# Paged attention behind three conditional layers: page numbers read two batches ahead on the SP queue, new values loaded in a batch's sixth step, output-weight loads in other steps

## The chip, the cores and the metric

The kernel runs on one core of one Trainium2 chip. The metric is the device time of one execution in microseconds (us). Before the change three runs took 1156.72, 1157.05 and 1160.14 us; their median is 1157.05 us. The profile was taken in an execution of its own.

## The reference

32 sequences ("batches") of 32 tokens pass through three layers that pick their weights by index, and then through attention over a paged cache. Only the attention is touched by the change:

```python
q = jnp.einsum('bsd,ed->bse', x, Wq).reshape(bsz, seqlen, HQ, D)   # 32 heads of 128
k = jnp.einsum('bsd,ed->bse', x, Wk).reshape(bsz, seqlen, HK, D)   # 8 key heads
v = jnp.einsum('bsd,ed->bse', x, Wv).reshape(bsz, seqlen, HK, D)
...
kc = k_cache[block_table].reshape(bsz, L, HK, D)                   # 16 pages of 32 keys each
vc = v_cache[block_table].reshape(bsz, L, HK, D)
...
scores = jnp.einsum('bqhd,bkhd->bhqk', q, k_all) * SCALE
scores = jnp.where(valid[:, None, None, :], scores, -1e+30)
probs = jax.nn.softmax(scores, axis=-1)
o = jnp.einsum('bhqk,bkhd->bqhd', probs, v_all)
return jnp.einsum('bse,de->bsd', o.reshape(bsz, seqlen, HQ * D), Wo)
```

`block_table[b]` lists the 16 cache pages of batch b. `k_all` and `v_all` are the cached keys and values with the 32 new ones behind them, 544 in all. Everything is float32.

## The kernel before

The first part (up to about 373 us) computes the three layers and the projections. The new queries, keys and values go to scratch arrays in DRAM (`q_d`, `k_d`, `v_d`). The attention then runs as one loop of 264 steps, n = 0 to 263. Step n belongs to batch b = n // 8 and key head g = n % 8. In each step TensorE (PE) computes the scores of (b, g) in two products (L1011 for nine pages, L1012 for seven pages and the new keys), one or two of the 32 head products of an output tile that is being finished (L1166, from n = 37 on), and the weighted values of step n - 8 (L1089; the constant LAG is 8). Until n = 36 some steps also hold a piece of the last value projection (L313), whose results are stored to `v_d`. VectorE, ScalarE and GpSimd turn scores into placed, transposed probabilities in between.

In this loop the order on every engine is the order in which the code is written (`manual_schedule`), the SP queue included. SP issues the DMAs of the keys, queries, new values, page tables and output weights, one after the other; an instruction of SP that waits holds back all that stand behind it. In the built program each DMA of SP also waits until the one issued eight places earlier has landed.

What SP does for batch b, before the change:

- Step 0: `load_queries(b, 1)` (`qt`, L229, the second half of the queries; its buffer is that of the batch before, so it waits for the last scores of batch b - 1). Then `load_new_values(b)` (`vn`, L265, four DMAs of 32 KB). Then `Picked(...)` for batch b + 1: it reads the first eight page numbers from the table in SBUF into registers of SP (eight register loads, L187). Then the new keys of batch b + 1 (`kt`, L224), and pages 0 to 11 of batch b + 1 (`kt`, L199, 128 KB each); after each of the first eight pages the next page number is read.
- Step 4: the first half of the queries of batch b + 1 (`qt`, L229; it waits for the scores of step 3), its inverse roots (`rq`, L235), pages 12 to 15 (L199), and the table of batch b + 2 (`pages`, L172, 64 bytes).
- Steps listed in `WO_AT`: one of the output weights' 32 loads (`wo`, L910). The first 16 bring the heads 0 to 19 (320 KB each), the other 16, in steps 40 to 55, the heads 20 to 31 (192 KB each). Load i of the first 16 holds a quarter of the rows of the heads h with h % 4 = i // 4, so the last four (12 to 15) are needed for heads 3, 7, 11 and so on. The first heads are used in step 37 (head 0), 38 (head 1) and 39 (heads 2 and 3).

Keys of batch b + 1 overwrite those of batch b - 1 (two buffers, `home_0` and `home_1`). The new values `vn` have two buffers too; `vn` of batch b is read in step 8b + 11. Cached values (`vt`, L253) are gathered by GpSimd on a queue of its own, in steps 0 to 3 of their batch, and first read in step 8b + 8.

Of the kernel before, what the change touches and what calls it, by code (L numbers as in the profile page):

```python
# [21 lines left out]
B, S, HID = 32, 32, 512  # L22
D, HQ, HK = 128, 32, 8
REP = HQ // HK
PAGES, PSIZE, NPP = 64, 32, 16
# [13 lines left out]
QUAD = 4  # L39
# [20 lines left out]
def cond_resid_kernel(  # L60
# [18 lines left out]
    nc = tc.nc  # L79
# [86 lines left out]
    pages_of = {}  # L166

    def load_table(b: int):

        pages_of[b] = const.tile([1, NPP], I32, tag="pages", name=f"pages_{b}", bufs=4)  # L170
        at = B + b * NPP
        nc.sync.dma_start(out=pages_of[b], in_=pick[:, at : at + NPP])  # L172
# [36 lines left out]
    def load_keys(b: int):  # L209

        pool = homes[b % 2]
        kt = pool.tile([P, NPP + 1, HK * PSIZE], F32, tag="kt", name=f"kt_{b}")
        kts[b] = kt
# [9 lines left out]
    def load_new_keys(b: int):  # L223
        nc.sync.dma_start(out=kts[b][:, NPP, :], in_=k_d[b])  # L224

    def load_queries(b: int, q: int):

        qts[b, q] = qp.tile([P, HALF * S], F32, tag="qt", name=f"qt_{b}_{q}")
        nc.sync.dma_start(  # L229
            out=qts[b, q], in_=q_d[b][:, q * HALF * S : (q + 1) * HALF * S]  # L230
        )

    def load_inverses(b: int):
        rqs[b] = const.tile([P, 2, QUAD], F32, tag="rq", name=f"rq_{b}", bufs=2)
        nc.sync.dma_start(out=rqs[b], in_=r_d[:, b * S : (b + 1) * S])  # L235

    def page_keys(b: int):
        return [kts[b][:, n, :] for n in range(NPP)]

    K_SHAPE = "a d x -> d (a x)"  # L240
# [8 lines left out]
    def load_value_chunk(b: int, c: int):  # L249
        if c == 0:  # L250
            vts[b] = homes[b % 2].tile([P, L // P, HK * D], F32, tag="vt", name=f"vt_{b}")
        at = b * (L // P) + c
        nc.gpsimd.indirect_dma_start(  # L253
            out=vts[b][:, c, :],
            out_offset=None,
            in_=v_cache,
            in_offset=bass.IndirectOffsetOnAxis(ap=v_idx[:, at : at + 1], axis=0),
        )

    def load_new_values(b: int):  # L260

        vn = vnp.tile([P, HK // QUAD, D], F32, tag="vn", name=f"vn_{b}")
        vns[b] = vn
        for u in range(QUAD):
            nc.sync.dma_start(  # L265
                out=vn[u * S : (u + 1) * S, :, :],
                in_=v_d[b * S : (b + 1) * S, :].rearrange("s (q u d) -> u s q d", u=QUAD, d=D)[u],
            )
# [53 lines left out]
    def store_values(vs, c: int, t: int, eng):  # L322
        c0 = (c - (HQ + HK) // REP) * HID
        eng.dma_start(out=v_d[t * P : (t + 1) * P, c0 : c0 + HID], in_=vs)
# [676 lines left out]
    def quad_of(b: int, g: int):  # L1001
        return b, g // QUAD

    def scores(b: int, g: int):
        kt, qt = kts[b], qts[quad_of(b, g)]
        kt4 = kt.rearrange("d n (h o) -> d n h o", h=HK)

        ps = ps_s.tile([P, 2 * L], F32, tag="s", name=f"s_ps_{b}_{g}")
        u = g % QUAD
        q = qt[:, u * REP * S : (u + 1) * REP * S]  # L1010
        nc.tensor.matmul(ps[:, first:L], q, kt4[:, :N_LOW, g, :], start=True, stop=True)  # L1011
        nc.tensor.matmul(  # L1012
            ps[:, L : first + LT], q, kt4[:, N_LOW:, g, :], start=True, stop=True
        )
        if u == 0:
            prs[quad_of(b, g)] = tp.tile([P, QUAD, LT], F32, tag="pr", name=f"pr_{b}_{g}")
        pr = prs[quad_of(b, g)][:, u, :]
        low = tp.tile([P, 1], F32, tag="low", name=f"low_{b}_{g}", bufs=4)

        nc.vector.tensor_tensor_reduce(  # L1020
            pr,
            ps[:, first : first + LT],
            mask,
            rqs[b][:, g // QUAD, u : u + 1],
            3.0e38,
            ALU.add,
            ALU.min,
            low,
        )
        return b, g, pr, low  # L1030

    def exponentials(b: int, g: int, pr, low):
        quad, u = quad_of(b, g), g % QUAD
        if u == 0:
            dens[quad] = tp.tile([P, QUAD], F32, tag="den", name=f"den_{b}_{g}", bufs=4)
        nc.scalar.activation(  # L1036
            pr, pr, AF.Exp, bias=low, scale=-1.0, accum_out=dens[quad][:, u : u + 1]
        )
# [97 lines left out]
    def flip_kept(n: int):  # L1136

        while kept and kept[0][3] <= n:
            b, q, o, _ = kept.pop(0)
            t, j = divmod(b, BT)  # L1140
            if (t, q) not in ots:
                i = (2 * t + q) % 3
                ots[t, q] = places[i].tile(
                    [P, HALF, P], F32, tag=f"ot_{i}", name=f"ot_{t}_{q}", bufs=1
                )
            nc.vector.transpose(  # L1146
                ots[t, q][:, :, j * S : (j + 1) * S],
                o.rearrange("p (k d) -> p k d", d=S),
            )
# [3 lines left out]
    def load_residual(t: int):  # L1153
        x3s[t] = tp.tile([P, HID], F32, tag="os", name=f"x3_{t}")
        nc.sync.dma_start(out=x3s[t], in_=x_d[t])
# [61 lines left out]
    FILLED = 37  # L1217
    EMPTY = tuple(n for n in range(LAG + 2, FILLED) if n % 2 == 0)
    EMPTY = EMPTY[: FILLED - len(fills)]
    filled, unstored = {}, {}  # L1220
    WO_AT = list(range(6, FILLED, 2)) + list(range(FILLED + 3, FILLED + 3 + REP * REP))

    def fill(n: int):
        if n < FILLED and n not in EMPTY:
            t, k = fills.pop(0)
            if k == 0:
                filled[t] = ps_p.tile([P, HID], F32, tag="f", name=f"qkv_{NCH - 1}_{t}")
            project_part(filled[t], NCH - 1, t, k)
            if k == KC - 1:
                unstored[n + 2] = copy_values(filled.pop(t), NCH - 1, t), NCH - 1, t, nc.sync  # L1230
# [8 lines left out]
    with tc.manual_schedule(engines=order):  # L1239
        for n in range(N + LAG):  # L1240
            b, g = divmod(n, HK)
            if n == FILLED + 2:
                pa.close()
                late = ctx.enter_context(tc.tile_pool(name="b_w", bufs=1))
                places.append(late)
                wos[1] = late.tile([P, LATE, HID], F32, name="wo_1")
            if BEGIN <= n <= N and n % (BT * HK) == 0:

                load_residual((n - BEGIN) // (BT * HK))
            if n < N:  # L1250
                if g == 0 and b >= 1:
                    load_queries(b, 1)
                    load_new_values(b)
                if g == 0 and 1 <= b < B - 1:
                    load_keys(b + 1)
                    keys = Picked(nc.sync, k_cache, pages_of.pop(b + 1), page_keys(b + 1), K_SHAPE)
                    load_new_keys(b + 1)
                    keys.transfer(slice(0, 12))
                if g < L // P and b >= 2:
                    load_value_chunk(b, g)  # L1260
                if g == QUAD and b < B - 1:
                    load_queries(b + 1, 0)
                    load_inverses(b + 1)
                    if b >= 1:
                        keys.transfer(slice(12, NPP))
                    if 1 <= b < B - 2:
                        load_table(b + 2)
                scored = scores(b, g)
                exponentials(*scored)
            flip_kept(n)  # L1270
            fill(n)
            if n in unstored:
                store_values(*unstored.pop(n))
            if n == QUAD + 1:
                load_new_values(0)
            if n in WO_AT:
                i, part = divmod(WO_AT.index(n), REP * REP)
                load_wo(i, *divmod(part, REP))
            if QUAD <= n < N + QUAD:
                bq, i = divmod(n - QUAD, HK)  # L1280
                q, j = divmod(i, QUAD)
                if j == 0:
                    gather_new(bq, q)
                if j == 2:
                    flip_new(bq, q)
                place(bq, q, j)
            share(n)
            if n >= LAG:
                values(*units[n - LAG])
            if n < N and g == HK - 1 and b < B - 1:  # L1290
                see_keys(b + 1)
            if n > N + QUAD:
                at = 4 * (n - N - QUAD - 1)
                finish(NT - 1, range(at, at + 4))
        assert not dens and not prs and not pos and not placed and not pns
        load_residual(NT - 1)
        flip_kept(N + LAG)
        finish(NT - 1, range(3 * QUAD, HALF))
        finish_by_halves(NT - 1)
# [76 lines left out]
```

## Time and profile before

| | us |
|---|---|
| median of the three runs | 1157.05 |
| the profiled execution | 1152.46 |
| its span, first to last instruction | 1150.4 |
| busy in the span: PE | 1127.8 |
| DVE | 805.5 |
| ACT | 751.8 |
| POOL | 553.1 |
| first scores of the attention (L1011) | 373.6 |
| mask of batch 5, 6, 7, 8 (L219, start) | 490.95, 514.59, 536.42, 559.52 |
| mask of batch 10, 11, 12, 13, 14 | 606.65, 628.48, 650.49, 674.34, 697.62 |

The mask of a batch is made once, at its beginning, so the distance between two masks is one batch: 21.8 to 23.9 us late in the loop, in a pattern that repeats every four batches (four output tiles' steps). The chain of waits that ended last runs through PE. Of the idle time of PE before L1012, 6.4 us in three waits ended with a DMA of cached keys; before L1011 it was 1.2 us. The SP rows of the timeline show the DMAs' issue alone: a row's duration is the time that issuing took, and register loads do not appear, so that their time is a gap between two rows.

### The profile page before, as it was taken

The page shows a single profiled execution, that of the slowest core. Times are in us where ns is not written, and L with a number is a line of the kernel's source. Part 1 is how long each engine was busy: PE and PEld are TensorE (multiplying, and loading weights), DVE is VectorE, ACT ScalarE, POOL GpSimd, SP SyncE. Part 2 cuts the span into 40 slices and gives each one's busy share as a digit, 9 for nine tenths or more (in the row PEclk, how much of TensorE's full clock was granted, in tenths as well). Part 3 has the DMA queues.
Part 4 walks back from the last instruction along what each step waited for, and adds up shares of the span by engine and source line. Part 5 has one row for each costly group of instructions (what it writes and reads, how often), then busy time and mean ns, then how long its engine had stood idle before and what let it go on. Part 6 is the DMA issues. An engine that isn't in the chain of part 4 may idle for free. (4 is left out here: it accounts for less than half of the span.)

```text
span 1150.4 us, 19414 instructions
## 1 busy us (share of the span) xinstructions
PE 1127.8 (98%) x5432; PEld 733.4 (64%) x5432; DVE 805.5 (70%) x1670; ACT 751.8 (65%) x1900; POOL 553.1 (48%) x709
## 2 busy tenths in 40 slices
PE   8999999999999988899999999999999999999998
PEld 5454444444444566677777777777777777777766
DVE  2510688897876577678868877877777777877861
ACT  1212378666666777767777877777777877787750
POOL 3410689898988434343344334533443444344410
PEclk9999999999999999999999999999999999999999
DMA  8998447656366499989766776776677767775700
GB/s 317 393 411 338 176 134 233 167 150 175 91 178 166 119 270 269 271 234 291 249 211 206 256 235 201 225 253 214 213 227 236 232 205 223 246 232 190 246 29 10
DMA packets 170510, 250.88 MB, mean 218 GB/s; under 512 B 31362, under 2 KB 130306, under 8 KB 164642
## 3 DMA queue, kind: packets, MB, share of 16 engines
q1 hardware_dynamic: 147586, 167.44, 47.0%
q0 software_dynamic: 19216, 69.35, 17.9%
q10 hardware_dynamic: 3600, 12.85, 3.2%
q8 instruction: 44, 0.72, 0.3%
q14 instruction: 64, 0.52, 0.1%
HBM read 220.07 MB, written 29.49 MB: 217 GB/s over the span
## 5 line engine op out<-in xcount | busy, mean ns | idle before, releaser
L1061 ACT COPY placed<-turned 32x512 f32<-32x512 f32 x539 | 332.1, 616 | 31.4 <-DVE turned L1049 23.3
L1089 PEld LDWEIGHTS o_ps<-vt,placed 128*128 128x128 f32 x2048 | 269.2, 193 | 115.4 <-issue 89.7
L1020 DVE CUSTOM_DVE_ANT_0 pr<-s_ps,mask,rq 128x544 f32<-128x544 f32 x256 | 200.6, 784 | 140.8 <-PE s_ps L1012 132.9
L1036 ACT ACTIVATE pr<-pr,low 128x544 f32<-128x544 f32 x256 | 191.7, 749 | 145.2 <-DVE low L1020 143.2
L1089 PE MATMUL o_ps<-vt,placed 128*128 128x128 f32 x2048 | 271.9, 276 | 3.2 <-DVE ot L1146 1.3
L1063 POOL COPY placed<-turned 32x512 f32<-32x512 f32 x268 | 162.9, 608 | 231.4 <-DVE turned L1049 177.0
L1166 PE MATMUL f_ps<-wo,ot 128*128 128x512 f32 x480 | 242.0, 595 | 3.5 <-issue 2.8
L1049 DVE STREAM_TRANSPOSE turned<-pr 128x512 f32<-128x512 f32 x256 | 178.7, 698 | 0.1
L1011 PE MATMUL s_ps<-kt,qt 128*128 128x288 f32 x512 | 175.4, 424 | 1.8 <-DMA kt<-in_k_cache_dram 1.2
L1012 PE MATMUL s_ps<-kt,qt 128*128 128x256 f32 x512 | 153.1, 381 | 6.8 <-DMA kt<-in_k_cache_dram 6.4
L253 POOL DMA_INDIRECT vt<-in_v_cache_dram,v_idx x128 | 126.9, 991 | 39.3 <-issue 23.5
L1012 PEld LDWEIGHTS s_ps<-kt,qt 128*128 128x128 f32 x512 | 97.3, 191 | 35.2 <-issue 7.8
L432 POOL TENSOR_TENSOR ra<-ra,rs 128x512 f32<-128x512 f32 x80 | 103.7, 1302 | 10.9 <-DVE rs L427 9.3
L1166 PEld LDWEIGHTS f_ps<-wo,ot 128*128 128x128 f32 x480 | 85.7, 190 | 31.7 <-issue 17.0
L1065 DVE COPY placed<-turned 32x512 f32<-32x512 f32 x217 | 94.5, 435 | 5.5
L1072 POOL COPY pq<-pr 128x128 f32<-128x128 f32 x64 | 18.4, 288 | 164.1 <-PE o_ps L1089 90.3
L1011 PEld LDWEIGHTS s_ps<-kt,qt 128*128 128x128 f32 x512 | 77.8, 192 | 18.2 <-DVE low L1020 10.8
L445 ACT ACTIVATE sq<-x 128x128 f32<-128x128 f32 x256 | 76.2, 300 | 16.2 <-DVE x L403 12.8
L542 ACT COPY r<-m 128x512 f32<-128x512 f32 x80 | 46.3, 580 | 55.2 <-PE m L387 54.2
L387 PE MATMUL m<-w_pair,x3t 128*128 128x512 f32 x160 | 75.2, 592 | 0.0
L387 PE MATMUL m<-t_pair,x_sums 128*128 128x512 f32 x160 | 75.2, 592 | 0.0
L387 PE MATMUL m<-w_pair,x_sums 128*128 128x512 f32 x160 | 72.2, 592 | 0.0
(128 smaller groups left out, 1218.2 us busy)
## 6 DMA issues: line engine op xcount, KB each, us to landing
kt<-in_k_cache_dram SPq DMA_DIRECT2D x512, 128.0 KB
wa<-in_w_adapt_dram SPq DMA_DIRECT2D x32, 1024.0 KB
q_d<-st SPq DMA_DIRECT2D x128, 128.0 KB
qt<-q_d SPq DMA_DIRECT2D x64, 256.0 KB
w_pair<-in_w_qkv_dram ACTq DMA_DIRECT2D x8, 1024.0 KB
wo<-in_w_o_dram SPq DMA_DIRECT2D x16, 320.0 KB
k_d<-st SPq DMA_DIRECT2D x32, 128.0 KB
kt<-k_d SPq DMA_DIRECT2D x32, 128.0 KB
```

What stands on the lines that cost most here:

```text
L253: nc.gpsimd.indirect_dma_start(out=vts[b][:, c, :], out_offset=None, in_=v_cache, in_offset=bass.IndirectOffsetOnAxis(ap=v_idx[:, at : at ...
L387: nc.tensor.matmul(ps, of[:, k], by[:, k], start=(not more and k == 0), stop=(k == KH - 1), skip_group_check=more,)
L432: nc.gpsimd.tensor_tensor(u.a, u.a, u.s, ALU.add)
L1011: nc.tensor.matmul(ps[:, first:L], q, kt4[:, :N_LOW, g, :], start=True, stop=True)
L1012: nc.tensor.matmul(ps[:, L : first + LT], q, kt4[:, N_LOW:, g, :], start=True, stop=True)
L1020: nc.vector.tensor_tensor_reduce(pr, ps[:, first : first + LT], mask, rqs[b][:, g // QUAD, u : u + 1], 3.0e38, ALU.add, ALU.min, low,)
L1036: nc.scalar.activation(pr, pr, AF.Exp, bias=low, scale=-1.0, accum_out=dens[quad][:, u : u + 1])
L1049: nc.vector.transpose(part, pr)
L1061: nc.scalar.copy(dst, src)
L1063: nc.gpsimd.tensor_copy(dst, src)
L1089: nc.tensor.matmul(po, pt[:, c, :], vt[:, c, g * D : (g + 1) * D], start=(c == 0 and q == 0), stop=(c == L // P - 1 and q == 1),)
L1166: nc.tensor.matmul(pfs[t][:, :HID], ots[t, h // HALF][:, h % HALF, :], wo(h), start=(h == 0), stop=(h == (HQ if t < NT - 1 else HALF) - 1),)
```

## The change

```diff
-    WO_AT = list(range(6, FILLED, 2)) + list(range(FILLED + 3, FILLED + 3 + REP * REP))
+    WO_AT = [6, 7, 11, 13, 14, 15, 17, 19, 21, 22, 23, 27, 29, 30, 31, 35]
+    WO_AT += range(FILLED + 3, FILLED + 3 + REP * REP)
...
                 if g == 0 and b >= 1:
                     load_queries(b, 1)
-                    load_new_values(b)
                 if g == 0 and 1 <= b < B - 1:
                     load_keys(b + 1)
-                    keys = Picked(nc.sync, k_cache, pages_of.pop(b + 1), page_keys(b + 1), K_SHAPE)
                     load_new_keys(b + 1)
+                    keys.dsts = page_keys(b + 1)
                     keys.transfer(slice(0, 12))
...
+                if g == QUAD + 1 and b >= 1:
+                    load_new_values(b)
+                if g == QUAD + 2 and b < B - 2:
+                    keys = Picked(nc.sync, k_cache, pages_of.pop(b + 2), range(NPP), K_SHAPE)
```

FILLED is 37, QUAD 4, NPP 16 and B 32. The first eight register loads for the keys of batch b + 2 now stand in step 6 of batch b, ahead of the step in which those keys are issued (step 0 of batch b + 1); the pages' destinations are filled in there. `vn` of batch b is loaded in step 5 instead of step 0. The first 16 output-weight loads stand in the steps listed: two in batch 0, four in batch 1, five in batch 2, four in batch 3 and one (step 35) in batch 4, where there were 1, 4, 4, 4 and 3. The second 16 stay in steps 40 to 55. On PE, DVE, ACT and POOL the instructions and their order are the same as before; only SP's order differs.

## The prediction

> **What bounds the kernel now.** First the page: which engine fills the span, and how full are the 16 DMA engines over it?
>
> ```profile
> span 1150.4 us, 19414 instructions
> ...
> PE 1127.8 (98%) x5432; PEld 733.4 (64%) x5432; DVE 805.5 (70%) x1670; ACT 751.8 (65%) x1900; POOL 553.1 (48%) x709
> ...
> DMA  8998447656366499989766776776677767775700
> ...
> q1 hardware_dynamic: 147586, 167.44, 47.0%
> q0 software_dynamic: 19216, 69.35, 17.9%
> ```
>
> TensorE leaves 1150.4 - 1127.8 = 22.6 us idle, so no change that only reorders SP can give more than about that. The DMA row is at 9 in slices 15 to 17 (403 to 489 us: batches 1 to 4) and at 6 or 7 in most of what follows. Whether SP's order matters can differ between these two stretches, so I read both. Second, PE's timeline, for the places where it stood still in the attention:
>
> ```profile
> 413.32 0.72 PE L1011 MATMUL s_ps<-kt,qt 128*128 128x288 f32 x2 [0.88 <-DMA kt<-in_k_cache_dram]
> 416.12 1.19 PE L1012 MATMUL s_ps<-kt,qt 128*128 128x256 f32 x2 [2.08 <-DMA kt<-in_k_cache_dram]
> ...
> 440.83 0.67 PE L1012 MATMUL s_ps<-kt,qt 128*128 128x256 f32 x2 [2.41 <-DMA kt<-in_k_cache_dram]
> ...
> 463.72 0.67 PE L1012 MATMUL s_ps<-kt,qt 128*128 128x256 f32 x2 [1.87 <-DMA kt<-in_k_cache_dram]
> ...
> 487.02 1.57 PE L1166 MATMUL f_ps<-wo,ot 128*128 128x512 f32 x2 [2.82 <-issue]
> ```
>
> These are steps 16, 24 and 32 (the first of batches 2, 3 and 4), where the last cached keys came late, and step 39. There the profile names no releaser. But it is the second head product of that step, head 3, which needs the last of the first 16 `wo` loads, and SP's rows show that one issued 4.3 us before. Third, SP's timeline, there and for one late batch:
>
> ```profile
> 482.66 0.35 SPq L910 DMA_DIRECT2D wo<-in_w_o_dram  x1
> ...
> 701.43 0.35 SPq L224 DMA_DIRECT2D kt<-k_d  x1
> 702.01 9.71 SPq L199 DMA_DIRECT2D kt<-in_k_cache_dram  x12
> 711.81 0.38 SPq L229 DMA_DIRECT2D qt<-q_d  x1
> ...
> 713.12 1.89 SPq L199 DMA_DIRECT2D kt<-in_k_cache_dram  x4
> 715.10 0.28 SPq L172 DMA_DIRECT2D pages<-in_pick_dram  x1
> 717.08 0.34 SPq L229 DMA_DIRECT2D qt<-q_d  x1
> 717.47 2.48 SPq L265 DMA_DIRECT2D vn<-v_d  x4
> 722.96 0.34 SPq L224 DMA_DIRECT2D kt<-k_d  x1
> ```
>
> Between `qt` and the new keys lie 2.48 us of `vn` issue and a gap of 722.96 - 719.95 = 3.01 us: the eight register loads, 0.38 us each. The keys could go 722.96 - 717.5 = 5.4 us earlier. Fourth, the windows, cut where PE resumed (columns: stretch, length, busy and count of PE, PEld, DVE, ACT, POOL, clock, DMA share, GB/s):
>
> ```profile
> 390.00:413.30 23.30, 21.94 (x126) 15.92 (x125) 15.27 (x34) 18.52 (x39) 13.34 (x23) 1.00 0.60 172
> 413.30:440.80 27.50, 22.02 (x124) 17.07 (x125) 18.05 (x39) 18.85 (x38) 10.81 (x18) 0.94 0.92 262
> 440.80:463.70 22.90, 20.47 (x122) 15.67 (x123) 17.66 (x38) 17.98 (x36) 8.92 (x14) 1.00 0.94 276
> 463.70:490.10 26.40, 23.42 (x127) 17.42 (x128) 16.37 (x36) 17.88 (x36) 8.37 (x13) 0.95 0.88 267
> ...
> 606.30:628.20 21.90, 21.90 (x130) 16.71 (x129) 18.17 (x39) 17.48 (x36) 9.31 (x15) 1.00 0.70 230
> ```
>
> Batches 2 to 4 keep the DMA engines 88 to 94% busy; batch 1 leaves 40% free; a late batch has PE busy for all of its 21.9 us. So there are two regimes: late, nothing that SP does is waited for; early, the keys wait partly for SP's order and partly for the DMA engines themselves.
>
> **What the stalls cost.** Each is measured from one step's L1011 to the next, against the same kind of step undisturbed. A step without a third product takes 404.77 - 402.70 = 2.07 us. Step 16: 418.81 - 412.44 = 6.37, lost 4.3 (2.96 of waiting, and matmuls that took about twice as long after it: granted clock 0.50 in 416 to 418). Step 24: 442.38 - 437.77 = 4.61, lost 2.5. Step 32: 465.27 - 461.14 = 4.13, lost 2.1. Step 39: 490.09 - 482.26 = 7.83 against 2.77 for a step with one head plus 0.86 for the second, lost 4.2. By the masks, batch 5 took 23.64 us where batch 9 took 23.28, and batch 7 23.10 where batch 11 took 22.01: 0.4 + 1.1 more. From batch 8 on the pattern repeats to 0.1 us. All of it is 14.6 us, the ceiling of the change.
>
> **The change, part by part.** *Register loads and `vn` out of step 0.* No issue is removed: 2.48 + 3.01 = 5.5 us of SP's time per batch move behind the table's load. In a late batch SP's work is `qt` 0.4, new keys and twelve pages 10.4, `qt` and `rq` 1.3, four pages 2.0, table 0.4, `vn` 2.5, registers 3.0 = 20.0 us of 21.8; it still fits, with 1.8 us to spare. There the last page was issued at 715.0 and read at 719.1 without a wait, so pages 3 to 5 us earlier give nothing: 0 for batches 8 to 31. The work that hides the moved `vn` is the six steps between 8b + 5 and 8b + 11 (six by 2.7 = 16 us; before eleven steps). Its buffer was last read in step 8b - 5, so no wait is added there.
>
> *A new wait.* The first register load waits for the table issued in step 4; before, it stood eight steps' worth of work later. In a late batch `vn` covers 2.5 us of the landing, and SP's spare 1.8 us and the 4.1 us of the pages' old lead cover more; I cost it at 0. Queued behind it are the second query half, the new keys and all pages, and `wo` and `v_d` stores early on. No row shows the table's landing. The nearest are the gathers of 512 KB, 3.9 to 8.7 us with a median of 6.5; as 64 bytes it should be near or below the lower one, but behind pages in a full queue it lands with them.
>
> *Step 16 (batch 1).* SP ended `vn` of batch 0 at 387.2. The register loads now follow (to 390.2), two `wo` (0.9), `qt` (0.4): new keys at 391.7 instead of 395.8, 4.1 us earlier, into engines that are 60% busy. Two `wo` that stood ahead of the last pages (405.3, 406.3) become one. The last page needs to land 3.7 us earlier (416.1 to 412.4). I take the whole 4.3 us back; the bounds are 2.5 (a slow step still follows) and 4.3.
>
> *Step 24 (batch 2).* Steps 13 to 15 put two `wo` and a `v_d` store ahead of the keys, and batch 2 has five `wo` instead of four. Bytes that must land from about 412.5 on: two `wo` 0.66 MB, `v_d` 0.26, two `qt` 0.52, seventeen key pieces 2.23, cached values 2.10, two more `wo` 0.66: 6.43 MB. At 262 GB/s for 0.92 busy, 0.285 MB per us, that is 22.6 us: 435.1, and 1.5 to 2.3 us for landing (the fastest gather, 3.9 us, less 0.52 MB at q0's 0.337 MB per us), so about 437. Without a stall step 24 would be ready near 433.2 (412.4 + 20.8). So about 3.7 us are waited, 1.2 more than before. Bounds: 2.5 back (if the weights' bytes are absorbed) and 2.5 more lost (with a slowed clock). I take -1.2. *Step 32:* four `wo` as before, pages started about 2.5 us earlier against its step; +1.0 of 2.1, bounds -1 and 2.1. *Step 39:* the last load moves from behind the four pages of batch 4 to before its `qt`, 482.66 to near 476 on the old clock; +4.2, bounds 2 and 4.2. *Step 40:* its keys follow three `wo` left by batch 3; -1.0, bounds -2 and 0. *Batches 5 to 7:* same `wo` as before, pages earlier: +1.4, bounds 0 and 1.5.
>
> One page speaks against all of this. The Trainium skill ("DMA: Bandwidth & Descriptors", section "Issuing engines are not separate DMA queues") says that DMAs from every engine run on the same 16 DMA engines and interleave, and that issuing differently saves only the sequencer's time. The rows agree for batches 2 to 4 (0.88 to 0.94 busy) and not for batch 1 (0.60). By that rule alone steps 24 and 32 would give nothing, and the sum would be 4.3 + 4.2 + 1.4 - 1.0 = 8.9 us; with SP's issue taken as the only limit it would be the 14.6 us.
>
> **The sum.** 4.3 - 1.2 + 1.0 + 4.2 - 1.0 + 1.4 = 8.7 us off the profiled 1152.46 (span 1150.4 and 2.1 around it): 1143.8. The median of the runs is 4.6 us above that execution; the same difference gives 1157.05 - 8.7 = **1148.4 us**.
>
> **The rivals.** *SP's issue was the only limit:* nearly all stalls vanish, 12 to 14.6 us, 1142.5 to 1145. For it: even in the full stretch the share dips to 0.58 and 0.72 at 426 to 430 while SP issues pages. Against it: 22 to 25 us of DMA work per batch in 21 us of PE work. *The stalls only move:* batches 2 to 4 take as long as their bytes, batch 1's gain is waited for again at step 24 or 28 (the query half now stands behind the register loads), and only step 39 or part of it remains: within 3.5 us of before, about 1155. Against it: batch 1's free 40%, 9 us. *The table's wait becomes the lock (slower):* SP sits at the first register load until the table lands, and every page of the next batch behind it. Place: step 6 of each batch. Late in the loop the table would be issued 14.4 us into SP's batch of 21.8, and before, the pages began 5.9 us after `qt`; so pages are later than now only if the table takes over 21.8 + 5.9 - 0.6 - 3.0 - 14.4 = 9.7 us, and PE waits only after 1 to 2 us more. At 12 us, 1 us in each of 24 batches, less 8.7: 1172. For it: in the full stretch pages landed 5.5 to 6.5 us after their issue. Against it: late the engines are 70% busy, and 600 to 606 us, where a batch's loads have ended, shows a share of 0.30.
>
> **How the numbers follow.** Forecast 60%, between 1145 and 1153; all stalls gone 17%; stalls moved 15%; lock 8%. The range takes in the second case and most of the third: 1142 to 1156. A difference under 0.3% (3.5 us, 1153.6 to 1160.5) is about what these runs can tell from none. The first two cases lie below it: faster 0.77, same 0.15, slower 0.08.
>
> **What would show it.** In the profile after: no wait of PE for `kt` at step 16 and none at head 3 of step 39; `qt` of step 0 followed at once by the new keys; a wait for `kt` of 1 to 4 us left at step 24; batches from 8 on as long as before to 0.1 us; a gap of about 3 us behind `vn` in step 6, longer in batches 1 to 4. I am wrong if step 16 still waits for keys, if step 24 doesn't, or if late batches lengthen.

## The result and the profile after

The change made the kernel slower. Six runs of the changed kernel took 1167.02 to 1174.56 us, median 1170.85; six runs of the kernel before, taken beside them, 1156.67 to 1160.14, median 1157.55. The ratio is 1.0113, with a 95% interval of 1.0088 to 1.0139: about 13 us lost, where the forecast was 8.7 us gained. One run of those reported below (1166.50 us, of e2_new_wo_alone) fell into a slower state and is left out of its figures. The profiled execution is the one of 1167.02 us. From its page, the span, the engines and the DMA row:

```profile
span 1165.2 us, 19419 instructions
...
PE 1133.3 (97%) x5432; PEld 734.2 (63%) x5432; DVE 804.5 (69%) x1670; ACT 751.5 (65%) x1900; POOL 552.8 (47%) x709
...
DMA  8998456646376688789775776677577766766610
```

TensorE is still busy nearly all the time, but its idle time grew from 22.6 to 31.9 us (1165.2 - 1133.3), and its busy time by 5.5 us, although the matmuls are the same. Of these 5.5 us, 1.5 lie in batches 0 to 7, where some matmuls run slowly after a long wait, as the rows below show; 3.4 lie in batches 8 to 31 and 0.5 ahead of the attention. Where it happened is told by two stretches of equal length in both kernels, in the view by windows (columns: stretch, length, busy time and count of PE, PEld, DVE, ACT, POOL, then the granted clock, the DMA share, GB/s). The kernel before:

```profile
374.00:562.00 188.00, 174.55 (x951) 128.04 (x950) 132.46 (x287) 137.31 (x282) 75.53 (x118) 0.98 0.83 240
562.00:1140.00 578.00, 575.83 (x3261) 428.54 (x3260) 438.41 (x934) 424.67 (x849) 224.23 (x335) 1.00 0.65 210
```

The changed kernel:

```profile
374.00:562.00 188.00, 167.20 (x898) 121.23 (x897) 125.20 (x271) 130.02 (x273) 69.35 (x108) 0.97 0.83 233
562.00:1140.00 578.00, 575.13 (x3260) 427.06 (x3260) 442.77 (x947) 433.08 (x866) 230.58 (x345) 1.00 0.65 213
```

In the first stretch (batches 0 to 7 of the kernel before) TensorE did 53 matmuls fewer in the same 188 us and lost 7.3 us of work; the DMA engines are as busy as before but moved 233 GB/s instead of 240. In the second stretch TensorE lost only 0.7 us of 578. So the added waiting lies in the first eight batches. Five of the longer waits in TensorE's timeline of the changed kernel there (in brackets: the wait, and what ended it):

```profile
426.47 0.72 PE L1011 MATMUL s_ps<-kt,qt 128*128 128x288 f32 x2 [1.17 <-DMA qt<-q_d]
...
439.94 1.30 PE L1011 MATMUL s_ps<-kt,qt 128*128 128x288 f32 x2 [3.65 <-DMA kt<-in_k_cache_dram]
...
454.43 0.72 PE L1011 MATMUL s_ps<-kt,qt 128*128 128x288 f32 x2 [2.20 <-DMA qt<-q_d]
...
481.26 1.30 PE L1011 MATMUL s_ps<-kt,qt 128*128 128x288 f32 x2 [5.45 <-DMA qt<-q_d]
...
543.14 0.72 PE L1011 MATMUL s_ps<-kt,qt 128*128 128x288 f32 x2 [2.05 <-DVE mask L219]
```

The waits at steps 16 and 39 are gone. New ones ended with `qt<-q_d`: the second half of the queries, at steps 20, 28 and 36 (step 4 of batches 2, 3 and 4). No such wait was there before. Step 24 waits longer than before (3.65 us; 2.41 before). Two rows show 1.30 us for a pair of products that takes 0.72 us elsewhere; the granted clock was 0.50 there, from 440 to 442 and from 481 to 483 us. The row at 543.14 (step 56) names VectorE, whose mask was done at 542.42; by the trace of the DMAs' landings the first query half of that batch, issued behind four `wo`, landed at 543.05. Step by step, from the start of L1011 in a step to that in the next, the two profiled executions differ like this (worked out from the two traces; minus is gained):

| steps | what waits there | after - before, us |
|---|---|---|
| 15, 16 | cached keys, batch 2 | -3.5 |
| 19, 20 | query half, batch 2 | +0.2 |
| 23 to 25 | cached keys, batch 3 | +2.7 |
| 27, 28 | query half, batch 3 | +1.8 |
| 32, 33 | cached keys, batch 4 | -1.5 |
| 35, 36 | query half, batch 4 | +7.0 |
| 39 | output weights, head 3 | -4.3 |
| 40 to 63 (batches 5, 6, 7) | query halves, keys, weights | +6.3 |
| batches 8 to 31 | (below) | +4.1 |

With 0.2 us in other steps these make the 13.0 us by which the attention became longer. Another 1.7 us lie ahead of it, where nothing was changed.

**Why the query half was late at step 36.** SP's timeline before, from the table of batch 5 to the keys:

```profile
458.55 0.28 SPq L172 DMA_DIRECT2D pages<-in_pick_dram  x1
460.06 1.15 SPq L910 DMA_DIRECT2D wo<-in_w_o_dram  x2
461.31 0.39 SPq L324 DMA_DIRECT2D v_d<-vs  x1
461.80 0.38 SPq L229 DMA_DIRECT2D qt<-q_d  x1
462.22 2.55 SPq L265 DMA_DIRECT2D vn<-v_d  x4
467.77 0.34 SPq L224 DMA_DIRECT2D kt<-k_d  x1
```

and after:

```profile
462.65 0.28 SPq L172 DMA_DIRECT2D pages<-in_pick_dram  x1
462.98 2.68 SPq L265 DMA_DIRECT2D vn<-v_d  x4
465.70 3.66 SPq L910 DMA_DIRECT2D wo<-in_w_o_dram  x2
469.47 0.38 SPq L324 DMA_DIRECT2D v_d<-vs  x1
469.90 0.43 SPq L910 DMA_DIRECT2D wo<-in_w_o_dram  x1
470.42 0.38 SPq L229 DMA_DIRECT2D qt<-q_d  x1
470.85 0.57 SPq L224 DMA_DIRECT2D kt<-k_d  x1
```

From the table to `qt` SP took 461.80 - 458.55 = 3.25 us before and 470.42 - 462.65 = 7.77 after. The row of 3.66 us for two `wo` holds the register loads between them. Before, `qt` was issued ahead of the four gathers of cached values (the first at 462.61). After, it came behind all four (465.56 to 469.61), three `wo` and a store of 256 KB. In the trace of the DMAs' landings it landed 5.3 us after its issue before, and 10.7 us after it now, at 481.12; TensorE resumed at 481.26. Meanwhile the DMA engines had had time to spare, as the windows of the changed kernel show:

```profile
462.00:464.00 2.00, 2.00 (x13) 1.47 (x11) 1.46 (x4) 1.95 (x6) 1.17 (x2) 1.00 0.91 269
464.00:466.00 2.00, 1.68 (x7) 0.66 (x5) 1.31 (x3) 1.96 (x4) 1.67 (x3) 1.00 0.17 50
466.00:468.00 2.00, 1.81 (x12) 1.71 (x13) 1.97 (x4) 0.93 (x3) 1.76 (x3) 1.00 0.58 131
468.00:470.00 2.00, 2.00 (x13) 1.50 (x12) 1.92 (x6) 1.46 (x3) 1.42 (x2) 1.00 1.00 265
```

While SP issued four small `vn` loads and read registers, the DMA share fell to 0.17 and 0.58. Behind that the loads came in one heap. The same place before (461 to 467 us, in three windows of 2 us) kept 0.97, 0.96 and 1.03.

### The profile page after: what moved, and what is told of

It reads as the page before. It is cut to its first block, busy times and chain, and to the rows that moved or that the text cites. A ratio compares the mean times of both kernels' runs of the same rounds, so it can differ in the third digit from the quotient of the medians.

```text
span 1165.2 us, 19419 instructions
## 1 busy us (share of the span) xinstructions
PE 1133.3 (97%) x5432; PEld 734.2 (63%) x5432; DVE 804.5 (69%) x1670; ACT 751.5 (65%) x1900; POOL 552.8 (47%) x709
## 5 line engine op out<-in xcount | busy, mean ns | idle before, releaser
L1011 PE MATMUL s_ps<-kt,qt 128*128 128x288 f32 x512 | 177.0, 428 | 16.3 <-DMA qt<-q_d 9.7
L1011 PEld LDWEIGHTS s_ps<-kt,qt 128*128 128x128 f32 x512 | 77.9, 192 | 33.9 <-issue 12.4
```

## The experiments

Theory A: the loss comes from the new steps of the output weights, which together with the value stores stand ahead of the query half. Theory B: it comes from moving the register loads and the new values. All ratios below are against runs of the kernel before on the same chip.

| run | median us (range) | before there | ratio [95% interval] |
|---|---|---|---|
| e1_old_wo | 1163.41 (1161.38 to 1165.95) | 1153.94 | 1.0087 [1.0062, 1.0111] |
| e2_new_wo_alone | 1156.35 (1145.84 to 1159.04) | 1153.94 | 1.0004 [0.9974, 1.0033] |
| e3_vn_alone | 1154.65 (1151.94 to 1160.34) | 1153.94 | 1.0011 [0.9992, 1.0031] |
| e4_registers_alone | 1165.89 (1163.17 to 1167.57) | 1153.94 | 1.0111 [1.0085, 1.0137] |
| r1_after_again | 1170.05 (1168.07 to 1170.98) | 1154.44 | 1.0145 [1.0127, 1.0164] |
| r2_undo_registers | 1156.01 (1151.53 to 1161.39) | 1154.44 | 1.0019 [1.0000, 1.0038] |
| r3_extra_registers | 1162.52 (1159.46 to 1164.64) | 1154.44 | 1.0076 [1.0058, 1.0093] |
| r4_after_gathers_later | 1167.06 (1163.22 to 1172.19) | 1154.44 | 1.0122 [1.0099, 1.0146] |
| t1_registers_table_early | 1161.62 (1154.31 to 1169.68) | 1156.46 | 1.0036 [1.0011, 1.0060] |
| t2_after_table_early | 1170.41 (1165.77 to 1174.07) | 1156.46 | 1.0114 [1.0084, 1.0143] |
| w1_weights_in_batch0 | 1154.50 (1150.97 to 1159.60) | 1156.46 | 0.9983 [0.9965, 1.0001] |
| w2_plus_first_registers | 1155.22 (1150.16 to 1159.06) | 1156.46 | 0.9979 [0.9961, 0.9996] |
| e4_again | 1165.90 (1162.37 to 1170.22) | 1154.21 | 1.0103 [1.0079, 1.0127] |
| t1_again | 1162.31 (1152.97 to 1166.50) | 1154.21 | 1.0052 [1.0026, 1.0078] |
| x5_early_table_old_values | 1162.93 (1160.59 to 1165.24) | 1154.21 | 1.0080 [1.0059, 1.0100] |
| x4_registers_from_batch7 | 1156.43 (1155.25 to 1163.47) | 1154.21 | 1.0033 [1.0017, 1.0050] |

### The parts by themselves

`e1_old_wo` is the changed kernel with the old steps of the output weights:

```diff
-    WO_AT = [6, 7, 11, 13, 14, 15, 17, 19, 21, 22, 23, 27, 29, 30, 31, 35]
-    WO_AT += range(FILLED + 3, FILLED + 3 + REP * REP)
+    WO_AT = list(range(6, FILLED, 2)) + list(range(FILLED + 3, FILLED + 3 + REP * REP))
```

> The change with the old list of output-weight steps (6, 8, ... 36), so that only the register loads and the new values are moved. Theory A (the loss comes from output-weight loads and value stores that now stand ahead of the second query half and the keys at a batch's beginning): the early loss of about 9 us by batch 8 goes, 1155 to 1161 us, and the wait for the second query half at steps 20, 28 and 36 shrinks below 1 us each. Theory B (moving the register loads and new values is itself the loss, because the pages are now issued while the cached values' gathers run): 1165 to 1172 us, with the waits at steps 20, 28 and 36 still there. Both expect the 0.4 to 0.6 us per four batches of the late loop to remain (3 to 4 us in all).

`e2_new_wo_alone` is the kernel before with the new list alone, the reverse of that diff.

> Before with the new list of output-weight steps alone. Theory A: slower, 1160 to 1168 us, since the loads of steps 13 to 15, 21 to 23 and 29 to 31 stand ahead of the queries and keys here too; late batches as before to 0.1 us. Theory B: 1153 to 1159 us, the stall at step 39 gone (4 us) and no new one.

`e3_vn_alone` is the kernel before with the new values in step 5:

```diff
                     load_queries(b, 1)
-                    load_new_values(b)
...
+                if g == QUAD + 1 and b >= 1:
+                    load_new_values(b)
```

> Before with the new values loaded in step 5 instead of step 0; register loads and output weights as before. Pages start 2.5 us earlier. Theory A: 1152 to 1158 us. Theory B: part of the late loss, about half of 0.55 us per four batches, and no loss early: 1157 to 1161 us.

`e4_registers_alone` is the kernel before with the first eight register loads in step 6:

```diff
-                    keys = Picked(nc.sync, k_cache, pages_of.pop(b + 1), page_keys(b + 1), K_SHAPE)
                     load_new_keys(b + 1)
+                    keys.dsts = page_keys(b + 1)
...
+                if g == QUAD + 2 and b < B - 2:
+                    keys = Picked(nc.sync, k_cache, pages_of.pop(b + 2), range(NPP), K_SHAPE)
```

> Before with the first eight register loads moved to step 6; new values and output weights as before. Pages start 3 us earlier, and the second query half stands behind the register loads, which wait for the table. Theory A: 1152 to 1159 us. Theory B: 1159 to 1166 us, with a wait of over 1 us for the second query half in at least one of the steps 20, 28 and 36.

The register loads alone cost as much as the whole change (1.0111). The new list alone and the new values alone change the median by less than can be told. Theory A falls as the main cause. Of Theory B only the register loads are left: e3 stayed at 1154.65 us where it asked for 1157 to 1161, and e1, at 1163.41, lies between the ranges of both theories. All four profiles lose in batches 1 to 8 only; from batch 9 on each batch takes as long as before to 0.01 us, so that the late loss of 3 to 4 us that both theories expected of e1 is not there.

The waits do not go the way the time goes. In e1 TensorE waits less than 1 us for the query half at steps 20, 28 and 36, as Theory A asked, and its profile is 13.2 us behind that of before at batch 8 all the same: it waits 3.87 us at step 39 and 5.03 us at step 59. In e2 the stall at step 39 shrank to 0.51 us, but 6.06 us are waited for cached keys at step 32, where Theory B expected no new stall.

In e4's trace SP stood at the first register load until the table had landed: SP's waits name this 29 times, 42.7 us in all. At the end of batch 2 the table was issued at 438.02 and landed at 439.82, and the loads ended at 442.5. The query half came 443.43 - 438.02 = 5.4 us behind the table; before it was 437.96 - 434.67 = 3.3. Theory C from here: the loads in step 6 hold SP for 3 to 4 us, ahead of output weights, value store and query half.

### The same again, one part undone, waits alone, gathers later

`r1_after_again` is the changed kernel once more.

> The changed kernel once more, on another run of the chip. Theory C (the eight register loads in step 6 hold SP for 3 to 4 us in front of the output weights, the value store and the second query half of the same batch, which then reach the full DMA engines together with the gathers; only the stretch up to batch 8 pays): ratio to before 1.008 to 1.014, and batches 8 to 31 as long as before to 0.1 us each, so that the 0.4 us at step 4 of every fourth late batch in the first profile belonged to that execution. Rival L (the register loads cost something in late batches too): the same 0.4 us at step 4 of batches 10, 14, 18, 22, 26, 30 again.

The loss came again, 1.0145 (just above Theory C's range), and again at steps 28 and 36 (waits of 3.81 and 5.46 us for `qt`). In batches 8 to 31 it was 0.9 us in all, 0.33 of it at batch 8, against 4.1 us in the first profile; the 0.4 us at step 4 of every fourth batch was not there. The same 0.4 us turned up later in the profiles of t1 (first run, not the second), t2, w1 and w2; w1 has nothing of the change but other steps for the first weights. So it comes and goes between executions of one kernel, and is not the change's; where it comes from stays open.

`r2_undo_registers` is the changed kernel with the register loads back in step 0:

```diff
                     load_keys(b + 1)
+                    keys = Picked(nc.sync, k_cache, pages_of.pop(b + 1), page_keys(b + 1), K_SHAPE)
                     load_new_keys(b + 1)
-                    keys.dsts = page_keys(b + 1)
...
-                if g == QUAD + 2 and b < B - 2:
-                    keys = Picked(nc.sync, k_cache, pages_of.pop(b + 2), range(NPP), K_SHAPE)
```

> The changed kernel with the first eight register loads back in step 0 of the batch; new values in step 5 and the new output-weight steps stay. Theory C: the loss goes with them, ratio to before 0.996 to 1.004. Rival (the three parts hurt only together): ratio above 1.006.

1.0019: the loss is gone with the one part. A long wait stays, in TensorE's timeline of this run:

```profile
437.28 1.04 PE L1011 MATMUL s_ps<-kt,qt 128*128 128x288 f32 x2 [2.81 <-DMA kt<-in_k_cache_dram]
...
454.92 1.30 PE L1011 MATMUL s_ps<-kt,qt 128*128 128x288 f32 x2 [5.28 <-DMA qt<-q_d]
```

So step 28's wait for the query half does not need the register loads; it is longer than with them (2.20 and 3.81 us in the two profiles of the change). The new values (step 21) and three `wo` (steps 21, 22, 23) stand right ahead of it there, and this gives back much of what steps 16 and 39 bring; with the new list alone (e2) the same wait was 1.08 us. At step 36, though, nothing is waited for: `qt` was issued at 468.11 and landed at 476.50, 8.4 us later, where the changed kernel took 10.7 and 12.0 us in its two profiles. TensorE also came to this batch later than in the changed kernel, by 2.9 and 1.7 us (the table at the end of the experiments).

`r3_extra_registers` is the kernel before with eight more register loads in step 6:

```diff
+                if g == QUAD + 2 and b < B - 2:
+                    Picked(nc.sync, k_cache, pages_of[b + 2], range(NPP), K_SHAPE)
```

> The kernel before with eight more register loads in step 6, whose values are not used; the eight of step 0 stay. Theory C (SP held in step 6 is the price): ratio 1.007 to 1.014, with PE waiting for the output weights at step 39 for 5 to 7 us, as where the loads were moved. Rival D (what hurts is that step 0 no longer has the pause of 3 us, so that pages run into the gathers): within 0.3% of before.

This run told something else than was meant. The values of the extra loads are not used, and in the built program the loads are gone; what is left is an empty instruction for each, 0.06 us apart, with the wait of the first one. So it is the wait for the table and half a microsecond more, and its ratio is 1.0076. The stall at step 39 grew to 5.31 us, as Theory C asked. SP's waits, of the kernel before (columns: waited for, us in all, times, longest):

```profile
SPq L229 <- PE s_ps L1012: 66.3, 30, 4.8
```

and of this run:

```profile
SPq L187 <- DMA pages<-in_pick_dram: 38.8, 29, 1.9
...
SPq L229 <- PE s_ps L1012: 8.3, 12, 1.9
```

A wait of 38.8 / 29 = 1.3 us per batch was enough. In the late batches it cost little (0.9 us in batches 8 to 31 in all): there SP had been waiting for TensorE at the query half anyway, 66.3 us in 30 waits in the kernel before, which are now 8.3 us.

`r4_after_gathers_later` is the changed kernel with the gathers one step later:

```diff
-                if g < L // P and b >= 2:
-                    load_value_chunk(b, g)
+                if 1 <= g <= L // P and b >= 2:
+                    load_value_chunk(b, g - 1)
```

> The changed kernel with the four gathers of cached values one step later (steps 1 to 4 of a batch instead of 0 to 3). Theory C with the gathers as the competitor: the query half lands before them, PE's waits for qt at step 4 of batches 2, 3 and 4 (1.2, 2.2 and 5.5 us in the first profile after) fall to a third or less in sum, and the ratio to before is at most 1.006. Rival (the bytes alone set the length of batches 2 to 4): the waits move to other steps and the ratio stays at 1.009 to 1.014.

The waits for `qt` at steps 20, 28 and 36 fell to 3.56 + 2.86 = 6.4 us from 9.3 in the run of the changed kernel on this chip, not to a third, and the ratio stayed at 1.0122. That gathers come first is a part of the delay, but moving them does not give the time back; the rival was nearer.

### Without the wait for the table, and two other lists

`t1_registers_table_early` is e4 with this besides:

```diff
-                    if 1 <= b < B - 2:
-                        load_table(b + 2)
+                    if b < B - 3:
+                        load_table(b + 3)
```

> Only the register loads are moved to step 6, as in the run of that part alone, but the table they read is loaded one batch earlier (step 4 of the batch before), so that it has landed long before. Theory W (the wait for the table is most of the price: SP may not issue until the table, and with it what stands ahead of it in the queue, has landed, and the DMA engines run low meanwhile; in the run with extra register loads the build had dropped the unused loads and kept their waits, and that alone gave 1.0076): ratio to before at most 1.005. Rival H (each microsecond for which SP is held in step 6 costs the same, waiting or loading; 2.7 us of the 3.5 to 4 are loads): ratio 1.006 to 1.010.

`t2_after_table_early` is the changed kernel with the same.

> The changed kernel with the table loaded one batch earlier. Theory W: ratio to before at most 1.006 and waits for qt at step 4 of batches 2 to 4 of less than 5 us in sum (9 to 11 us in the two profiles of the change). Rival H: ratio 1.008 to 1.012, waits of 6 us or more.

`w1_weights_in_batch0` is the kernel before with `WO_AT = [4, 5, 6, 7, 12, 13, 14, 15, 16, 18, 20, 22, 24, 26, 28, 30]` for the first sixteen.

> The kernel before with the first sixteen output-weight loads in steps 4 to 7, 12 to 15 and then every second step from 16 to 30, so that four lie in batch 0 and none in batch 4; nothing else moved. If batches 2 to 4 are long because of what SP's queue and the DMA engines have to do there, the wait at step 39 (4.2 us) goes and step 16 gives 0 to 2 us: ratio 0.994 to 0.998. Rival (what is taken from step 39 is waited for elsewhere, as in the run of the change's new list alone): 0.999 to 1.003.

`w2_plus_first_registers` is the same with the first register loads for batch 2 in step 6 of batch 0 and all others in step 0:

```diff
+                    if b >= 2:
-                    keys = Picked(nc.sync, k_cache, pages_of.pop(b + 1), page_keys(b + 1), K_SHAPE)
+                        keys = Picked(nc.sync, k_cache, pages_of.pop(b + 1), page_keys(b + 1), K_SHAPE)
+                    keys.dsts = page_keys(b + 1)
...
+                if n == QUAD + 2:
+                    keys = Picked(nc.sync, k_cache, pages_of.pop(2), range(NPP), K_SHAPE)
```

> The same with the register loads for the keys of batch 2 alone in step 6 of batch 0, where the table landed long ago and SP has room. The wait at step 16 (4.3 us) goes as well, as wherever SP reached those keys 3 us earlier: ratio 0.990 to 0.996. Rival (the gain of step 16 is waited for again at step 24): no better than the run without it.

For the loads alone the early table took most of the price away (1.0036); for the whole change it took nothing (1.0114). There, the four `vn` loads stand between table and register loads and cover the landing: SP's waits in the changed kernel have no line for L187 at all, so that there was nothing to remove. In the full change theory W falls and rival H holds.

The two lists win little. w1's profile has no wait at steps 16 and 39, which together are 8.5 us, and these in their place:

```profile
437.90 1.09 PE L1011 MATMUL s_ps<-kt,qt 128*128 128x288 f32 x2 [2.24 <-DMA kt<-in_k_cache_dram]
...
466.18 1.19 PE L1012 MATMUL s_ps<-kt,qt 128*128 128x256 f32 x2 [3.64 <-DMA kt<-in_k_cache_dram]
```

What is saved at steps 16 and 39 is waited for again at steps 24 and 32. Both ratios miss the gains expected (0.994 to 0.998 and 0.990 to 0.996). At 0.9983 and 0.9979 the two are the fastest versions here, but only the second one's interval lies below 1, by less than the 0.3% that counts as a difference.

### What settles it

`e4_again` and `t1_again` are the two runs of the moved loads, with the late and the early table, on one chip.

> The register loads alone in step 6 once more, now beside the same with an early table on one chip. All theories: ratio to before 1.008 to 1.014.

> The register loads alone in step 6, table loaded one batch earlier, once more. Theory W (alone, the wait for the table is most of the price): at most 1.006 and at least 0.004 below the run with the late table on this chip. Rival H (time of SP is time of SP, waiting or loading): within 0.003 of it.

1.0103 and 1.0052, or 12 and 6 us: about half goes with the wait, the rest stays (two thirds in the first pair of runs, 1.0111 and 1.0036, which were on different chips). T1_again is 0.0051 below e4_again, as theory W asks, and still above the kernel before, so the loads have a price of their own. SP's waits of e4_again:

```profile
SPq L187 <- DMA pages<-in_pick_dram: 41.0, 29, 2.9
```

In t1_again this line is not there. In both the largest stall of TensorE is the one at step 39 for the last output weights (2.82 us before). In the timeline of e4_again:

```profile
493.86 2.04 PE L1166 MATMUL f_ps<-wo,ot 128*128 128x512 f32 x2 [6.00 <-issue]
```

and of t1_again:

```profile
492.82 2.05 PE L1166 MATMUL f_ps<-wo,ot 128*128 128x512 f32 x2 [7.05 <-issue]
```

In e4_again the last of the first sixteen, in step 36, was issued at 490.14, where it had been 482.66 (2.0 us of this lie ahead of the attention), and landed at 493.77. So the loads alone act at step 39, through the output weights; in the full change they act at step 36, through the query half.

`x5_early_table_old_values` is t2 with the new values back in step 0.

> The changed kernel with the table one batch earlier and the new values back in step 0; register loads in step 6 and the new list of output-weight steps stay. Theory V (with the early table the price of the change is SP's time between the table and the second query half: 2.5 us for the new values and 2.7 us of loads are too long together, each alone is bearable): ratio to before at most 1.006, at least 0.005 below the changed kernel with the early table (1.0114 on another chip). Rival (loads and the new list together are enough): 1.008 or more.

1.0080, with an interval from 1.0059 to 1.0100: the rival, just. The loads and the new list are enough for most of the loss. Whether the new values in step 5 add the rest to 1.0114 can't be told, since the intervals overlap and the chips differ.

`x4_registers_from_batch7` is the changed kernel, in which the register loads move to step 6 from batch 7 on only:

```diff
+                    if b < 8:
+                        keys = Picked(nc.sync, k_cache, pages_of.pop(b + 1), page_keys(b + 1), K_SHAPE)
                     load_new_keys(b + 1)
...
-                if g == QUAD + 2 and b < B - 2:
+                if g == QUAD + 2 and 7 <= b < B - 2:
```

> The changed kernel with the register loads in step 6 only from batch 7 on; before that they stay in step 0. All theories that put the loss into batches 1 to 8: as without moved loads, 0.998 to 1.005. Rival (late batches pay for the moved loads too): above 1.006.

1.0033, beside 1.0019 for all of them in step 0: 23 of the 30 moves cost nothing that can be told. The price is paid by the moves of batches 0 to 6. How far each profiled execution stands behind that of before at the start of a batch, counted from its own first scores (us, worked out from the traces; the profiled execution of before was 4.6 us below its median, so every row is a few us too high; those of the change were 3.8 and 2.0 us below theirs, that of r2 2.4 above):

| start of batch | 3 | 4 | 5 | 7 | 8 | 31 |
|---|---|---|---|---|---|---|
| the change, first profile | 0.5 | 1.5 | 2.6 | 5.3 | 8.9 | 13.0 |
| the change again | -2.0 | 2.7 | 4.1 | 6.4 | 14.1 | 15.0 |
| registers back in step 0 (r2) | -0.7 | 4.4 | -1.1 | 1.6 | 5.0 | 5.9 |
| registers moved from batch 7 (x4) | -2.1 | 3.8 | -2.2 | -0.1 | 3.5 | 4.4 |
| registers alone (e4_again) | -1.4 | 2.3 | 5.3 | 8.0 | 12.1 | 12.1 |
| registers alone, early table (t1_again) | -2.4 | 0.6 | 5.9 | 6.7 | 7.4 | 8.2 |

The rows part in batch 4: with the loads in step 0 it gains 5.5 to 6 us by the start of batch 5 (step 39's stall goes and step 36 does not wait); with the loads in step 6 it loses 1 to 5. In batches 5 to 7, however, the rows with the loads in step 0 lose 6.1 us (r2) and 5.7 (x4), as the changed kernel does (6.3 and 10.0); the new list alone (e2) loses 0.1 there and the new values alone (e3) 2.4. So the loss of these three batches is not shown to come from the register loads, and what makes it stays open.

## Why the prediction was wrong

*Step 16: 4.3 us back.* Right: 3.5 came back.

*Step 24: 1.2 us lost.* Right in sign, too small: 2.7 lost, just beyond its bound of 2.5.

*Step 32: 1.0 back.* Right: 1.5.

*Step 39: 4.2 back, step 40: 1.0 lost.* Right for the first, 4.3. Step 40 lost nothing, it gained 0.4.

*Batches 5 to 7: 1.4 back.* Wrong: 6.3 lost, and 10.0 in the second profile (14.1 - 4.1). Here I had only compared the output weights' number and taken the keys' earlier issue as a gain. The same loss without the moved loads (r2, x4) leaves its cause open.

*Late batches: 0.* Right, by r1, e4 and x4 (0.9, 0.8 and 0.9 us); the 4.1 us of the first profile did not come again in the second, and come and go in other runs.

*The new wait: "I cost it at 0".* Right for this change: the new values cover it, and an early table brought nothing (t2). With the loads moved alone it is half of the price (e4_again, t1_again, r3), from 1.3 us of waiting in a batch.

*"5.5 us of SP's time per batch move behind the table's load ... it still fits, with 1.8 us to spare".* This is the step that failed. I worked it out for a late batch, and there the runs bear it out (x4). But the gain was all in batches 1 to 7, and there SP also issues two or three `wo` and a value store between table and query half, where the late batch has none. In the sum there is no term for what stands behind the moved loads at that place. The text even named it ("Queued behind it are the second query half, the new keys and all pages, and `wo` and `v_d` stores early on") and gave it no price. The runs showed, in the place of this missing term, 9.0 us of waiting for the query half at steps 20, 28 and 36 (0.2 + 1.8 + 7.0), 7.0 of them at step 36. That the register loads there are the cause of the slower kernel is shown by r2 and x4: without the early moves the ratio falls from 1.0145 to 1.0019 on the same chip, and to 1.0033 on another. In the profiles it is step 36 that goes with them; the wait at step 28 and the loss of batches 5 to 7 stay, and use up what steps 16 and 39 give. How the 13 to 17 us divide among loads, new values and new list in the full change is not settled: each of the last two alone gives no difference, all three together more than the loads alone or as much.

*The time in step 0 was not all lost time.* I took the 3.0 us of register loads in step 0 as a delay of the keys. But each DMA of SP waits for the one eight places earlier, and once the pages are reached sooner they wait there instead. SP's waits ahead of the pages, from 374 to 562 us in the kernel before:

```profile
SPq L199 <- DMA kt<-in_k_cache_dram: 0.6, 2, 0.4
```

and in the changed kernel:

```profile
SPq L199 <- DMA wo<-in_w_o_dram: 8.9, 8, 3.1
SPq L199 <- DMA kt<-in_k_cache_dram: 2.0, 2, 1.3
SPq L199 <- DMA kt<-k_d: 1.6, 2, 0.9
SPq L199 <- DMA qt<-q_d: 1.4, 1, 1.4
SPq L199 <- DMA v_d<-vs: 1.4, 2, 1.0
```

From 562 us on they rose from 9.6 to 36.3 us, all for earlier pages, and there nothing was lost by it: x4 has 33.7 us of them. Early, about 15 us are waited where 0.6 were before, more than half of it for output weights; with the loads back in step 0 (r2) it is 9.9. That part of the old 3.0 us was cover is read from these lines; no run took the gate away.

*The rivals.* The one that came nearest is "the stalls only move": it said that the gain is "waited for again at step 24 or 28 (the query half now stands behind the register loads)". The place was right, and its mechanism, the query half behind the register loads, acted at step 36; at step 28 the wait came without them too (r2, x4). Its price was not: I let it give back what batch 1 gained, 4.3 us, and by the table of steps 18.0 us were given back (0.2 + 2.7 + 1.8 + 7.0 + 6.3). The rival on the slow side, the table as a lock, had the wrong place: it was priced for late batches, from 9.7 us of landing on, and the table landed in 1.4 to 3.5 us. At the early place waits of 1.3 us for the table, without any moved load, were enough for 1.0076 (r3). The row I gave in its favour was misread as well: the pages of batches 3 to 5 landed 2.0 to 6.7 us after their issue, not 5.5 to 6.5.

*The signs.* Most of those I had named came true: no wait for keys at step 16, none at step 39, 3.65 us at step 24, the query half followed at once by the new keys. None of them looked at when the query half itself would land, so they could all hold while the time went the other way.

*The rule on DMA queues.* The Trainium skill ("DMA: Bandwidth & Descriptors", section "Issuing engines are not separate DMA queues") says that the DMAs of all issuing engines share 16 engines and interleave. The runs agree: the second query halves of batches 2, 3 and 4 landed 9.3, 7.7 and 10.7 us after their issue in the changed kernel, where SP issued them among or behind GpSimd's gathers, and 5.8, 6.4 and 5.3 us before. The sum by that rule, 8.9 us gained, was as wrong as mine, since it too has no term for a load that comes late in the heap. The order is a part of it only: with the gathers one step later (r4) the ratio stayed at 1.0122.

## What to carry to other kernels

Cost a moved instruction at its new place in the stage where the gain is expected, not in the stage where the queue is easiest to read: ask there what stands behind it, and who waits for that. Time that an issuing engine spends where it would have waited in any case is free, as in the late batches here; the same time where TensorE needs the very next loads was paid for with about 1% of the kernel. Read a register load of freshly loaded data as a wait: loading the data a round earlier took back half of the price or more of the moved loads alone, and nothing that can be told of that of the full change; leaving them where the queue waits in any case took back nearly all.

## What was not expected of the hardware

One register load of SP took 0.27 us in the median, and the first of a row 0.45 to 0.73 in most rows; a row of eight took 2.6 to 3.0 us of SP's time. When the loads were held back, they also took longer to land: between 410 and 560 us the query halves took 5.3 us from issue to landing in the median before (longest 6.5), and 6.6 after (longest 10.7). Small changes of order make the runs of one kernel differ more: the moved loads with the early table ran between 1152.97 and 1166.50 us (t1_again), the kernel before on the same chip between 1149.71 and 1156.80. Why they do is not shown.

The matmuls after a wait ran slowly where the wait was long: 1.30 us for the pair of products behind 3.65 and 5.45 us (granted clock 0.50), 0.72 behind 1.17 and 2.20 (changed kernel). The Trainium skill ("TensorE: Matmul & The Clock Gate", section "Part 1: The HAM clock gate") puts the fall to half the clock after about 3.4 us of idling; these four rows agree, while in the kernel before a pair took 1.19 us behind two shorter waits of 0.88 and 2.08 us close together, and in r2 one took 1.04 us behind a wait of 2.81, so the rows alone give no threshold.
